# Agent attention on one core: v found and convolved one block further ahead, and the next image's moments with the third block

## The chip, the core and the metric

The kernel runs on one NeuronCore of a Trainium2 chip. The metric is the device time of one execution in microseconds. The engines are named as in the profile: PE multiplies matrices (PEld loads its weights), DVE is the vector engine, ACT the scalar engine, POOL is GpSimd, and SP issues DMAs. Matmul results lie in PSUM, everything else in SBUF. Each engine works through its own queue strictly in order; semaphores tie the queues together.

## The reference

Four layers, each `x = x + layer(groupnorm(x))`, on x of 32 images x 192 channels x 56 x 56 in fp32. Only the first layer is changed here, an attention through 49 "agents" with six heads of 32 channels:

```python
qkv = xf @ Wqkv + bqkv                       # xf: the normed image, 3136 pixels x 192
agent = q pooled 8x8                         # 49 agents
agent_attn = softmax(agent @ k.T * scale + pos_bias)   # over the 3136 pixels
agent_v = agent_attn @ v
q_attn = softmax(q @ agent.T * scale + agent_bias)     # over the 49 agents
out = q_attn @ agent_v + depthwise_conv3x3(v)
x = x + out @ proj_w + proj_b
```

The other layers (an RWKV scan, a shift with a 3 x 3 filter, a global convolution through spectra) follow it and are the same in both kernels.

## The kernel before

**Tiling.** `attention` (L365) takes the 32 images one after the other (loop over `b`, L759). The 56 x 56 pixels of an image are cut into four blocks of columns, 16, 16, 16 and 8 wide (`WIDTHS`); `j` counts them. The 192 channels lie as 128 and 64, and the 64 are folded by image halves onto 128 partitions, so each tensor is a pair (`_a`, `_c`).

**Pieces of work.** For the next image: `moments` (L433) takes the statistics and the 8 x 8 sums from the raw image, all on DVE (L438 to L461: `bn_stats`, then the reductions `by_x` at L447, `pool_a` at L450, `fours` at L455); `spread_of` and `scaling` make the group norm's scale of them; `normed` (L522) writes the normed block `xs_a`, `xs_c` on ACT; `find_agents` and `seen` (L495, L508) make the agents and what they see.

For a block: `find_v` (L538) computes v on PE and copies it on ACT into the padded images `v_a`, `v_c` (L546, L554) and into a flat tile. `convolve` (L560) applies the 3 x 3 filter: the centre tap on ACT (L570), the other eight as `scalar_tensor_tensor` on DVE (L572), for both tiles. Its right column needs the next block of v. `weigh` (L577) makes the scores of the 294 head-agent rows in three parts on PE (L585, L586), their row maxima `low` on DVE (L587) and the exponentials `pr` on ACT (L589). `turn_v` (L595) and `turn` (L608) transpose v and the exponentials through PE (L604, L617), with ACT copying (L605, L620). `gather` (L623) multiplies the two (L632, copied at L634) and `settle` (L637) turns the result and adds its halves (L641, L643, L645). `join` (L647 to L665) puts the four blocks together, almost all of it on DVE.

Then for each block `ask` (L669: scores on PE at L677 and L678, row maxima, subtraction and normalization on DVE at L681 to L694, exponential on ACT at L690), `turn_back` (L704, L708), `answer` (L712: L717, L722 on PE, sums with the convolved v on DVE at L719, L723) and `project` (L725, with matmuls in `_Pairs` at L834 to L847).

**What sets the order.** The order is that in which the functions are called, but a scheduler then moves instructions within each engine's queue by what it takes to be ready; the queues are fixed when the program is built. In the first loop over `j` (L766 to L781) the calls for a block are `weigh(j)`, `turn_v(j)`, `gather(j-1)`, `find_v(j+2)`, `turn(j)`, `settle(j-1)` and `convolve(j+1)`; after the last block come the next image's `moments`. In the second loop, over `t` = 1 to 5 (L788 to L812), `ask(t)`, `turn_back(t-1)`, `project(t-2)` and `answer(t-1)` run beside the next image's `normed`, `find_v(0)`, `find_v(1)` (at `t` = 3 and 4) and `convolve(0)`.

**PSUM.** All of this shares four tiles of two banks each (L379, L386). A matmul group that needs a tile waits until the copy or reduction that reads the tile's former contents is done.

**Words used.** low(j) are the three row maxima of block j; ask(1), turn(3) and so on are the calls for that block.

## Time and profile before

| | us |
|---|---|
| median of three runs | 12294.04 (12291.52 to 12297.86) |
| the profiled execution | 12294.66 |
| its span on the core | 12292.8 |
| PE busy | 11329.2 (92%) |
| DVE busy | 10836.4 (88%) |
| ACT busy | 6205.0 (50%) |

The span has the filter of the last layer first (until about 160 us), then the attention until about 4840 us, the scan in the middle and the spectra at the end. L653, one instruction an image, gives the period: from the 11th to the 12th image it runs at 1741.47 and 1888.23 us. One image in the trace, 1741.47 to 1888.24, has PE busy for 141.4 us, DVE for 127.4 and ACT for 81.2.

How to read what follows: a row of the timeline gives start, duration, engine, line, operation, output and inputs, the number of instructions merged, and in brackets the idle time ahead of it with what ended it. DVE's durations overlap their successors' by some 0.08 us, so sums are made of differences of starts. A row of the stretches gives the busy time of PE, PEld, DVE, ACT and POOL with counts, then the clock granted to PE (1.00 is full), the share of the DMA engines and GB/s.

### The profile page before, as it was taken

The numbers are of one execution on the slowest core, as the hardware profiler recorded it, in microseconds if no ns is written. First come the engines' busy times: TensorE is split into PE (matmuls) and PEld (weight loads), VectorE is DVE, ScalarE is ACT, GpSimd is POOL, SyncE is SP. The second block draws the span as 40 slices with busy tenths as digits, with TensorE's granted clock in tenths as the row PEclk, the third lists the DMA queues.
The fourth block names the chain that finished last, engine by engine and source line by source line (L and its number), as shares of the span: only waits on it lengthen the run. The fifth ranks groups of instructions, "written<-read, shape, count | busy, mean of one in ns | idle before, by whom it ended". The sixth has DMA issues, their size and how long they took to land. (4 is left out here: it accounts for less than half of the span.)

```text
span 12292.8 us, 164375 instructions
## 1 busy us (share of the span) xinstructions
PE 11329.2 (92%) x62734; PEld 7107.7 (58%) x62734; DVE 10836.4 (88%) x15489; ACT 6205.0 (50%) x11808; POOL 2250.7 (18%) x2228
## 2 busy tenths in 40 slices
PE   7999999999999999788888888888999999999999
PEld 3555555655555555333333333336777777777777
DVE  6888888888888887999999999997888888888888
ACT  3555555555555554566666666663333333333333
POOL 0000000000000000655555555551000000000000
PEclk9999999999999999999999999999999999999999
DMA  2111111111111111244344433442111111111111
GB/s 69 40 42 46 52 41 40 40 40 40 40 40 40 42 50 44 75 103 100 95 97 103 101 94 97 103 101 65 44 41 45 41 44 42 44 42 44 42 43 29
DMA packets 930055, 719.69 MB, mean 59 GB/s; under 512 B 770325, under 2 KB 807236, under 8 KB 920124
## 3 DMA queue, kind: packets, MB, share of 16 engines
q1 hardware_dynamic: 919020, 683.39, 21.7%
q10 hardware_dynamic: 10240, 25.70, 0.8%
q8 instruction: 500, 8.19, 0.3%
q14 instruction: 295, 2.42, 0.1%
HBM read 403.47 MB, written 240.65 MB: 52 GB/s over the span
## 5 line engine op out<-in xcount | busy, mean ns | idle before, releaser
L572 DVE SCALAR_TENSOR_TENSOR o<-v_a,att_w,o 128x896 f32<-128x896 f32 (+1 forms) x1024 | 1053.8, 1029 | 418.6 <-ACT v_a L546 291.5
L1763 ACT COPY y<-ps 64x252 f32<-64x252 f32 (+1 forms) x2376 | 808.2, 340 | 1135.0 <-PE ps L1757 1104.8
L1681 PE MATMUL ps<-fixed,real 84*84 84x112 f32 x6144 | 1090.9, 259 | 0.0
L1681 PE MATMUL ps<-fixed,imag 84*84 84x112 f32 x6144 | 1089.5, 259 | 0.0
L1688 ACT COPY z<-ps 84x448 f32<-84x448 f32 x768 | 405.6, 528 | 1218.5 <-PE ps L1681 1217.0
L1086 POOL MEMSET f<- 128x1 f32 x96 | 8.9, 99 | 4726.3 <-DMA st_c<-st 4721.3
L1681 PEld LDWEIGHTS ps<-fixed,real 84*84 84x84 f32 x6144 | 784.0, 153 | 134.2 <-issue 95.8
L1681 PEld LDWEIGHTS ps<-fixed,imag 84*84 84x84 f32 x6144 | 763.8, 153 | 0.0
L1079 ACT ACTIVATE q<-q 128x784 f32<-128x784 f32 x384 | 328.2, 855 | 802.5 <-DVE q L1074 633.1
L834 PE MATMUL ps<-sq,fixed 128*128 128x392 f32 x512 | 297.3, 743 | 428.6 <-ACT sq L1157 428.6
L572 DVE SCALAR_TENSOR_TENSOR o<-v_c,att_w,o 128x448 f32<-128x448 f32 (+1 forms) x1024 | 635.0, 620 | 5.1
L585 PE MATMUL ps<-xs_a,gk_a 128*98 128x448 f32 (+1 forms) x1536 | 637.1, 495 | 0.0
L589 ACT ACTIVATE pr<-ps,low 98x896 f32<-98x896 f32 (+1 forms) x384 | 352.3, 918 | 559.9 <-DVE low L587 559.9
L586 PE MATMUL ps<-xs_c,gk_c 125*98 125x448 f32 (+1 forms) x1536 | 631.6, 492 | 0.0
L1547 POOL TENSOR_TENSOR mat<-tap,tap 114x114 f32<-114x114 f32 x96 | 40.8, 425 | 3166.1 <-PE ps L1607 2313.2
L677 PE MATMUL ps<-gq_a,xs_a 128*112 128x294 f32 x1792 | 602.8, 417 | 19.2 <-DVE pq L682 19.2
L1698 PE MATMUL ps<-z,fixed 84*114 84x448 f32 x1536 | 608.8, 539 | 0.0
L834 PE MATMUL ps<-x,weights 128*128 128x392 f32 x1536 | 577.4, 519 | 27.5 <-DVE bv L1108 14.2
L678 PE MATMUL ps<-gq_c,xs_c 125*112 125x294 f32 x1792 | 594.5, 412 | 0.0
L1655 PE MATMUL re<-y,fixed 128*84 128x420 f32 (+1 forms) x1152 | 532.3, 543 | 8.7 <-ACT y L1763 7.6
L1655 PE MATMUL im<-y,fixed 128*84 128x420 f32 (+1 forms) x1152 | 526.9, 538 | 0.0
L690 ACT ACTIVATE pq<-pq 112x1176 f32<-112x1176 f32 x224 | 265.3, 1184 | 498.9 <-DVE pq L682 376.0
(367 smaller groups left out, 29245.2 us busy)
## 6 DMA issues: line engine op xcount, KB each, us to landing
x<-x SPq DMA_DIRECT2D x576, 392.0 KB
x<-x SPq DMA_DIRECT2D x512, 196.0 KB
x<-x SPq DMA_DIRECT2D x192, 399.0 KB
out_x<-x SPq DMA_DIRECT2D x384, 196.0 KB
x<-in_x SPq DMA_DIRECT2D x32, 1568.0 KB
x<-x SPq DMA_DIRECT2D x32, 1568.0 KB
x<-in_x SPq DMA_DIRECT2D x64, 392.0 KB
rd<-rd ACTq DMA_DIRECT2D x128, 196.0 KB
```

The lines of the kernel that those rows point to most:

```text
L572: nc.vector.scalar_tensor_tensor(dst, tap(i), dww[:, t, i : i + 1], dst, ALU.mult, ALU.add)
L585: mm(ps[P2, h, :n], g[:, cols], xs_a[j][:, px], start=True, stop=False)
L586: mm(ps[P2, h, :n], gk_c[0:KC, 2 * j + h, cols], xs_c[j][0:KC, px], start=False, stop=True)
L589: nc.scalar.activation(pr[:, :, :n], ps[P2, :, :n], AF.Exp, bias=low[:, j, p : p + 1], accum_out=sums[:, j, p : p + 1])
L677: mm(ps[:SUB, i, :HA], xs_a[j][:, px], g, start=True, stop=False)
L678: mm(ps[:SUB, i, :HA], xs_c[j][0:KC, px], gq_c[0:KC, 2 * j + (q + i) // ns], start=False, stop=True)
L834: mm(out, aa, srcs[t][h], start=True, stop=False)
L1655: nc.tensor.matmul(ps[:, : n * 84], f2[:, i, :], y[:, i0 : i0 + n].rearrange("p g s u -> p (g s u)"), start=True, stop=True)
L1681: nc.tensor.matmul(ps[:84, i * 2 * S : (i + 1) * 2 * S], part[:, i0 + i].rearrange("p s u -> p (s u)"), f3[:, m, :], start=(m == 0), stop= ...
L1688: nc.scalar.copy(z[:, i0 : i0 + n].rearrange("p g m w -> p (g m w)"), ps[:84, : n * 2 * S])
L1698: nc.tensor.matmul(got, f4[:, m, :], z[:, i0 : i0 + n, m, :], start=(m == 0), stop=(m == 1))
L1763: nc.scalar.copy(y[64 * m : 64 * m + 64, 2 * g0 + i : 2 * (g0 + n) : 2], got[64 * i : 64 * i + 64, :, :, m, :])
```

## The change

v of the next image is found for three blocks rather than two before its loop begins, its block 0 is transposed there, and its blocks 0 and 1 are convolved (the second call stands at `t` = 5). Within the loop, `turn_v` runs one block ahead of `turn`, `find_v` is left for block 3 alone, `convolve` runs two blocks ahead, and the moments are called with block 2 rather than block 3. The same instructions work on the same data.

```diff
     v, o = {0: find_v(0), 1: find_v(1)}, {}
-    o[0] = convolve(0)
+    vT = {0: turn_v(0, v[0])}
+    v[2] = find_v(2)
+    for j in range(2):
+        o[j] = convolve(j)
...
-            vT = turn_v(j, v[j])
             if j > 0:
-                halves = gather(j - 1, *turned[j - 1])
-            if j + 2 < NK:
-                v[j + 2] = find_v(j + 2)
-            turned[j] = turn(j, prs), vT
+                halves = gather(j - 1, turned[j - 1], vT[j - 1])
+            if j + 1 < NK:
+                vT[j + 1] = turn_v(j + 1, v[j + 1])
+            if j == 0:
+                v[3] = find_v(3)
+            turned[j] = turn(j, prs)
             if j > 0:
                 settle(j - 1, halves, got)
-            if j + 1 < NK:
-                o[j + 1] = convolve(j + 1)
-            elif more:
+            if j + 2 < NK:
+                o[j + 2] = convolve(j + 2)
+            elif more and j + 2 == NK:
                 mv, pools = moments(nxt)
-        halves = gather(NK - 1, *turned[NK - 1])
+        halves = gather(NK - 1, turned[NK - 1], vT[NK - 1])
...
             if more and t == 4:
                 o[0] = convolve(0)
                 normed(nxt, rs, nb, 3)
+            if more and t == 5:
+                vT[0] = turn_v(0, v[0])
+                v[2] = find_v(2)
+                o[1] = convolve(1)
```

## The prediction

> **What bounds the kernel now.** I read the page first, then one image in stretches, then PE's and DVE's rows in the stretches where PE is not full.

> ```profile
> span 12292.8 us, 164375 instructions
> PE 11329.2 (92%) x62734; PEld 7107.7 (58%) x62734; DVE 10836.4 (88%) x15489; ACT 6205.0 (50%) x11808; POOL 2250.7 (18%) x2228
> PE   7999999999999999788888888888999999999999
> DVE  6888888888888887999999999997888888888888
> ```

> The diff touches attention alone, some 250 to 4840 us: slices 2 to 16, PE at 9, DVE at 8. The image correction L653 runs once an image, at 1741.47 and 1888.23 in the trace, so an image takes 146.8 us; 32 of them make the stage. One image, busy times of PE, PEld, DVE, ACT, POOL, then the clock granted to PE:

> ```profile
> 1741.47:1745.87 4.40, 1.88 (x13) 1.44 (x13) 4.40 (x10) 0.34 (x2) 0.00 (x0) 0.94 0.00 0
> 1745.87:1752.47 6.60, 6.56 (x30) 5.08 (x32) 6.60 (x10) 3.77 (x4) 0.00 (x0) 0.52 0.01 2
> ...
> 1808.77:1827.77 19.00, 19.00 (x87) 10.10 (x85) 12.84 (x19) 10.31 (x22) 0.00 (x0) 1.00 0.83 258
> ...
> 1845.97:1861.27 15.30, 14.71 (x111) 9.42 (x110) 15.30 (x25) 8.61 (x18) 0.00 (x0) 1.00 0.01 1
> 1861.27:1870.27 9.00, 9.00 (x96) 7.87 (x94) 9.00 (x21) 4.93 (x13) 0.00 (x0) 1.00 0.01 2
> ```

> PE is full from weigh(0) to ask(0). It is empty at the head of turn_back(0), and runs the 6.6 us after that at half clock (0.52). DVE is full from j = 1 to the end of the weighing, and empty for a third of j = 0. PE's rows at the two idle places:

> ```profile
> 1742.30 0.98 PE L468 MATMUL ps<-mv,att_k 128*128 128x1 f32 x8
> 1745.79 4.69 PE L704 MATMUL ps<-att_k,pq 112*98 112x112 f32 x24 [2.52 <-DVE f L658]
> ...
> 1806.09 1.02 PE L834 MATMUL ps<-o,att_w 128*128 128x224 f32 x4 [1.06 <-DVE o L719]
> ```

> The rest of PE's idle time is 0.63 us ahead of ask(1), 0.59 at gather(1), 0.34 and 0.23 at two turn_backs: 5.4 us an image. DVE's rows:

> ```profile
> 1825.03 2.34 DVE L572 SCALAR_TENSOR_TENSOR o<-v_a,att_w,o 128x896 f32<-128x896 f32 x2 [5.89 <-ACT v_a L546]
> ...
> 1866.48 0.61 DVE L587 TENSOR_REDUCE low<-ps 98x1 f32<-98x448 f32 x1
> 1867.01 1.15 DVE L438 BATCH_NORM_STATS2 st_a<-x 128x6 f32<-128x448 f32 x2
> ...
> 1870.31 3.37 DVE L447 TENSOR_REDUCE by_x<-x 128x392 f32<-128x3136 f32 x1
> ...
> 1877.21 0.75 DVE L681 TENSOR_REDUCE mx<-ps 112x12 f32<-112x588 f32 x1
> ```

> Two things to see. First, DVE idles 5.89 us for block 2 of v. Second, most of the moments run after the last low, from 1867.01 to 1877.21, when PE needs nothing of DVE: it does gather(2), turn(3), gather(3) and the first part of ask(0), without a gap until 1880.4. They are nearly hidden there.

> **The change, part by part.** No instruction is added or dropped but a few of waiting; the sums of work stay. What counts is DVE's queue, which the order of the changed kernel's instructions shows.

> *1. find_v(2) and turn_v(0) ahead of weigh(0).* The 5.89 us, and 0.20 at 1811.8, go from DVE: 6.1 us.

> *2. Moments with block 2.* In the new order all of the moments but a one-row memset stand ahead of block 3's last two lows. What stood after the last low and now stands before it: bn_stats and aggregates 1867.01 to 1870.31, 3.30; L447 3.27 and 1.70; L450 0.76; L455 0.91; L458 0.13; in all 10.1 us (starts subtracted in the timeline, L645 left out).

> *3. So the last low comes later.* From 1798.77, where the taps of block 0 go on once v's block 1 is there, to 1867.01 DVE was busy 61.93 of 68.24 us. Its chain keeps this start. The last low ended at 1867.0; now 1867.0 - 6.1 + 10.1 + 0.2 (semaphore steps) = 1871.2. ACT's exponential behind it takes 0.1 + 0.6, and of turn(3)'s 12 transposes nine wait for it, 0.83: the settle behind them starts at 1872.7, where it was 1869.82. **PE's price: 2.9 us.** Part of it falls earlier, at j = 0: the first low(0) now stands behind fifteen of convolve(1)'s sixteen taps, some 7 us after PE has its scores. This state has rows already, in the first image, where low(0) stands behind a whole convolve:

> ```profile
> 201.58 0.87 PE L604 MATMUL ps<-att_k,v 128*112 128x128 f32 x6 [0.79 <-ACT once L518]
> 203.34 0.87 PE L604 MATMUL ps<-att_k,v 128*112 128x128 f32 x6 [0.89 <-ACT vT L605]
> ```

> After it ACT's queue (L516, L518, three exponentials of 0.99, two L605 of 0.68, find_v(3)'s six copies 1.90, L620 0.54: 7.4 us) is longer than PE's own 6.2 us (turn_v 1.36, find_v(3) 2.62, turn 2.19), so 1.3 to 1.9 us of the 2.9 are seen here and the rest, 1 to 1.6 us, at turn(3). They are not added: DVE's queue sets the sum.

> *4. The ask.* DVE is now idle when ask(0) begins, but that does not help. PE waits for a PSUM tile that the second subtraction of ask(1) frees. From the row maximum of ask(0)'s last pair to that subtraction DVE took 1881.50 to 1892.41, 10.9 us. In the new order the join's three long steps (L660 0.87, L664 1.40, L665 0.21) stand inside this stretch, and one row sum (1.29) is out of it: 11.8 us by its sixteen rows. The maximum was 1.5 us late behind PE and will be 0.9 us late behind that row sum. Net 0.3 us later. I keep the half clock as it is. Behind it DVE has 2.5 us less to do, which takes the 0.23 at turn_back(1).

> *5. DMAs and queues.* No issue is moved but with its function; the next image's 2.35 MB (1568 and twice 392 KB) land in 1808.77:1827.77 (share 0.83), before the earlier moments would need them (some 1855). SP and POOL have nothing else here.

> Sum for an image: 2.9 + 0.3 - 0.2 = 3.0 us. In the first image the scheduler had already put these moments ahead (162 to 177 us), and DVE's chain there has hardly an idle place (1.0): 0. The last image has no moments: about 1 us by j = 0. **30 x 3.0 + 1 = 91 us.** The profiled execution took 12294.66 us (span 12292.8, 1.9 around it), the median of the runs is 12294.04: 12294.7 + 91 = 12386.

> *Unknown costs.* Whether turn(3)'s new wait also throws the clock: the nearest rows are 1.06 us (L834: clock 1.00 after it) and 2.52 us (0.52 after it, for 6.6 us). Mine is 1 to 1.6, nearer the first: 0; the other end is half of 6.6, so +3.3 us an image, at most +100. The new DVE waits in the chain, for find_v(2)'s and find_v(3)'s copies, come out within 0.2 to 0.8 us of it: 0 to +1 us, taken 0.2. Should the ask's wait shrink by a few tenths and the clock lose less: -1.7 us (one half of the 6.6 us); taken 0.

> The row at 1745.87 has half clock after 2.52 us of idle. [...]

> **Rivals.** *Faster: the ask's wait goes.* For it: moments are off DVE when ask(0) begins, and DVE is up to 3 us late there now (1877.21 against the first pair's end near 1874.3). If DVE needed under 9.3 us (PE's own work from that pair to turn_back(0)) in place of 11.8, then 0.63 + 2.52 and the half clock (6.6 x 0.48 = 3.2) would go: -6.3 + 2.9 = -3.4 us, 31 times: 12190. Against: DVE's order is fixed, and a start with an empty queue does not shorten what stands behind the last pair.
> *No change:* DVE's 4.0 us net delay of the last low is taken up. PE's slack there is only 0.85 us (1868.76 against the exponential's end, 1867.91). It needs the tile waits and the ask to give back some 3 us: 12295, give or take 25.
> *Slower still:* the wait at turn(3) throws the clock: 12386 + 50 to 100, 12440 to 12490.
> That the change does not do what it says is excluded by the order of its instructions.

> **How the numbers follow.** Forecast as summed (12335 to 12430) 0.55; slower still 0.15; no change, within 0.2% (25 us, about what a measurement of this kernel can tell from none) 0.12; faster 0.18. So faster 0.18, same 0.12, slower 0.70. The range, 12280 to 12490, leaves out most of the faster case (0.16) and a little above.

> **What would show it.** Right: an image of about 149.8 us; no 5.89 at L572; L447 ahead of the last L587; DVE idle before the first L681; PE waiting 1 to 1.6 us for ACT's pr at L617 of block 3 and under 1 us twice at L604 of j = 0; 2 to 3.5 us still idle ahead of turn_back(0). Wrong: no wait at that L617, or full clock after turn_back(0).

## The result and the profile after

The changed kernel takes **12415.1 us** (median of four runs, 12403.0 to 12416.2) where the kernel before took 12293.7 beside it (12291.5 to 12297.9): ratio **1.0096, interval 1.0079 to 1.0114**. It is slower by 121 us; the forecast was 12386, slower by 91. The profiled execution took 12414.3 us.

The head of the page after; compare span, PE's and DVE's busy time, and slices 2 to 16:

```profile
span 12412.3 us, 164446 instructions
...
PE 11388.9 (92%) x62734; PEld 7121.4 (57%) x62734; DVE 10869.1 (88%) x15489; ACT 6177.0 (50%) x11808; POOL 2285.2 (18%) x2228
...
PE   6999999999999999888888888888999999999999
...
DVE  5888888888888888899999999997888888888888
```

Both engines do the same instructions in the same number, and the page looks as before. The time has to be looked for in one image. The timeline of PE after, where PE idles in an image or has to wait for ACT (the image whose ask(0) begins at 1474.86 and ends with the next ask(0) at 1624.38):

```profile
1495.16 1.02 PE L468 MATMUL ps<-mv,att_k 128*128 128x1 f32 x8 [2.48 <-DVE pq L682]
1497.19 3.04 PE L704 MATMUL ps<-att_k,pq 112*98 112x112 f32 x16 [1.01 <-DVE pq L682]
...
1514.46 1.74 PE L704 MATMUL ps<-att_k,pq 112*98 112x112 f32 x16 [0.99 <-ACT pqT L708]
1516.43 1.77 PE L842 MATMUL ps<-o,att_w 128*128 128x448 f32 x4 [0.23 <-ACT pqT L708]
...
1561.15 1.02 PE L544 MATMUL ps<-xs_a,att_w 128*128 128x448 f32 x2 [0.23 <-ACT vT L605]
...
1577.60 1.86 PE L604 MATMUL ps<-att_k,v 128*112 128x128 f32 x12 [0.79 <-ACT once L518]
...
1622.16 0.38 PE L617 MATMUL ps<-att_k,pr 98*112 98x98 f32 x2 [0.53 <-ACT pr L589]
1622.78 0.97 PE L617 MATMUL ps<-att_k,pr 98*112 98x98 f32 x9 [0.23 <-ACT pr L589]
```

The last three rows are the price in the weighing: at j = 0 and at turn(3). The rows at 1514 and 1516, in and behind turn_back(1), and the one at 1561, where find_v(2) waits for a copy of turn_v(0), are new and were not forecast. The 0.59 at gather(1) and the 0.63 ahead of ask(1) are gone. The timeline of DVE after, end of the weighing and beginning of ask:

```profile
1613.01 3.36 DVE L447 TENSOR_REDUCE by_x<-x 128x392 f32<-128x3136 f32 x1
...
1618.23 0.85 DVE L450 TENSOR_REDUCE pool_a<-by_x 128x49 f32<-128x392 f32 x1
1619.00 0.99 DVE L455 TENSOR_REDUCE fours<-by_x 64x49 f32<-64x196 f32 x2
1619.91 0.61 DVE L587 TENSOR_REDUCE low<-ps 98x1 f32<-98x448 f32 x1
1620.55 0.20 DVE L458 TENSOR_TENSOR pool_c<-fours 64x49 f32<-64x49 f32 x1
1620.68 1.14 DVE L587 TENSOR_REDUCE low<-ps 98x1 f32<-98x448 f32 x2
...
1627.99 0.77 DVE L681 TENSOR_REDUCE mx<-ps 112x12 f32<-112x588 f32 x1 [2.82 <-PE ps L678]
```

The moments stand ahead of the last lows, the 5.89 us at L572 is gone, and DVE now idles ahead of ask(0), where it is of no use.

To place the time I cut every image at three starts on PE: ask(0), turn_back(0), weigh(0). All figures are means in us over images 5 to 27 (counted from 0), except the period, a mean over the 29 intervals between the second ask(0) and the 31st. "Taps to last low" is DVE's chain of step 3 of the prediction, with the idle time in it. "Half" is time at half clock in an image.

| kernel | time | period | ask(0) to turn_back(0) | to weigh(0) | to next ask(0) | taps to last low (idle) | half | first ask(0) at |
|---|---|---|---|---|---|---|---|---|
| before | 12293.7 | 146.80 | 22.01 | 62.97 | 61.81 | 68.32 (6.09) | 6.5 | 254.2 |
| after | 12415.1 | 150.43 | 22.33 | 69.82 | 58.36 | 72.39 (0.23) | 6.4 | 272.2 |
| moments alone | 12683.8 | 159.28 | 24.09 | 63.43 | 71.76 | 78.47 (6.09) | 18.1 | 252.2 |
| v ahead alone | 12312.8 | 147.60 | 22.33 | 69.63 | 55.64 | 69.61 (1.07) | 5.9 | 249.1 |
| convolve late | 12493.6 | 153.66 | 24.21 | 69.54 | 59.84 | 73.20 (1.07) | 12.2 | 254.2 |
| moments with block 3 | 12400.2 | 150.20 | 22.33 | 70.40 | 57.46 | 71.27 (0.23) | 9.9 | 266.0 |

Wherever v is ahead, turn_v(0) and find_v(2) (1.36 and 4.76 us of PE) have moved from the third stretch to the second. Less these 6.12 us, the change costs 2.7 us in the weighing, 0.3 in the ask and 0.7 between turn_back(0) and weigh(0). The whole: the first ask(0) comes 18.0 us later, the next 31 intervals add 110.1 (3.1, 29 times 3.63, 1.6), and behind the last ask(0) 8.6 us are given back: 119.5 us of span.

### The profile page after: what moved, and what is told of

It reads as the page before. It is cut to its first block, busy times and chain, and to the rows that moved or that the text cites. A ratio compares the mean times of both kernels' runs of the same rounds, so it can differ in the third digit from the quotient of the medians.

```text
span 12412.3 us, 164446 instructions
## 1 busy us (share of the span) xinstructions
PE 11388.9 (92%) x62734; PEld 7121.4 (57%) x62734; DVE 10869.1 (88%) x15489; ACT 6177.0 (50%) x11808; POOL 2285.2 (18%) x2228
## 5 line engine op out<-in xcount | busy, mean ns | idle before, releaser
L572 DVE SCALAR_TENSOR_TENSOR o<-v_a,att_w,o 128x896 f32<-128x896 f32 (+1 forms) x1024 | 1055.3, 1031 | 235.1 <-ACT o L570 127.4
L572 DVE SCALAR_TENSOR_TENSOR o<-v_c,att_w,o 128x448 f32<-128x448 f32 (+1 forms) x1024 | 636.8, 622 | 5.1 <-ACT v_c L557 2.4
```

The costliest lines, as they stand in the source:

```text
L572: nc.vector.scalar_tensor_tensor(dst, tap(i), dww[:, t, i : i + 1], dst, ALU.mult, ALU.add)
```

## Experiments

My theory was that DVE's queue up to the last low sets the weighing, and that the tile freed by the second subtraction of ask(1) sets the start of turn_back(0). The rivals were that finding v early, or convolving it early, is itself what costs, and that moments cost nothing wherever they stand.

### The moments alone

```diff
-            elif more:
+            if more and j + 2 == NK:
                 mv, pools = moments(nxt)
```

This edit is made to the kernel before.

> The kernel before with the moments alone called with block 2; v, its turning and its convolution stay where they were, so DVE keeps its 5.89 us idle at L572. Theory (DVE's queue up to the last low sets the end): all 10.1 us of moments now stand ahead of the last low and nothing is taken out for it, so the last low comes 10.1 us later, 0.85 us of that is PE's slack, and with the ask's +0.1 an image takes some 9 to 10 us more: 30 images, 12560 to 12600 us. Rival (the moments are hidden wherever they stand, and early v is what costs): 12294, give or take 25.

Measured: 12683.8 us, ratio 1.0316 (1.0298 to 1.0333), slower by 388 us. DVE's chain grew from 68.32 to 78.47 us, by the 10.1 us of moments that the theory names; the rival that moments are hidden anywhere is dead. But the time is 84 us beyond my range. The timeline of PE and the stretches of this run at turn(3) show why (the columns of the stretches are busy PE, PEld, DVE, ACT, POOL, then the granted clock):

```profile
1680.23 0.57 PE L617 MATMUL ps<-att_k,pr 98*112 98x98 f32 x2 [6.97 <-ACT pr L589]
```

```profile
1671.00:1680.00 9.00, 2.24 (x48) 2.05 (x48) 8.95 (x12) 0.95 (x3) 0.00 (x0) 0.88 0.00 0
1680.00:1685.00 5.00, 4.58 (x19) 3.11 (x19) 2.19 (x10) 3.13 (x10) 0.00 (x0) 0.50 0.00 0
1685.00:1700.00 15.00, 15.00 (x74) 10.96 (x74) 9.59 (x12) 3.09 (x4) 0.00 (x0) 0.90 0.01 2
```

PE waits 6.97 us in one place, and what follows, turn(3), gather(3) and the head of ask(0), runs at half clock. From turn(3)'s first transpose to ask(0) takes 3.7 us instead of 1.8, and the ask 24.09 instead of 22.01. That is the mechanism of the prediction's rival "slower still", here as a fact.

### v ahead alone

```diff
     vT = {0: turn_v(0, v[0])}
     v[2] = find_v(2)
-    for j in range(2):
-        o[j] = convolve(j)
+    o[0] = convolve(0)
...
-            if j + 2 < NK:
-                o[j + 2] = convolve(j + 2)
-            elif more and j + 2 == NK:
+            if j + 1 < NK:
+                o[j + 1] = convolve(j + 1)
+            if more and j + 1 == NK:
                 mv, pools = moments(nxt)
...
                 vT[0] = turn_v(0, v[0])
                 v[2] = find_v(2)
-                o[1] = convolve(1)
```

> The changed kernel with convolution and moments back where they were: find_v(2) and turn_v(0) ahead alone. The last lows stand after the first L447 of the moments but ahead of the second one, L450 and L455. Theory (DVE's queue): 6.1 us out, 6.7 in ahead of the last low, within PE's slack of 0.85: nothing for the weighing; what is left is the ask's 0.3 and, if it comes with this order, the PSUM tile of turn_back(1) (1.0 to 1.6): 12320 to 12350 us. Rival (finding and turning v early is itself what costs, whatever the moments do): 12390 to 12415.

Measured: 12312.8 us, ratio 1.0014 (1.0005 to 1.0024). The weighing costs nothing (55.64 and 6.12, against 61.81), the ask 0.3, the stretch behind turn_back(0) 0.5. The rival is dead: v ahead by itself costs 17 us, 7 less than the least I had expected.

### The convolution late

```diff
-    for j in range(2):
-        o[j] = convolve(j)
+    o[0] = convolve(0)
...
-            if j + 2 < NK:
-                o[j + 2] = convolve(j + 2)
-            elif more and j + 2 == NK:
+            if j + 1 < NK:
+                o[j + 1] = convolve(j + 1)
+            if more and j + 2 == NK:
                 mv, pools = moments(nxt)
...
-                o[1] = convolve(1)
```

> The changed kernel with the convolution one block ahead only, as before; v ahead and the moments with block 2 stay. The low lines of j=0 then come without fifteen taps ahead of them, so the 1.57 us stall at j=0 goes. Theory (DVE's queue sets the sum; the same work stands ahead of the last low): what is not waited for at j=0 is waited for at turn(3), an image takes as long as in the changed kernel; only the first image may be up to 18 us shorter: 12395 to 12420 us. Rival (the taps ahead of low(0), that is the convolution two blocks ahead, are the price): 1.57 us an image less, some 12345 to 12365.

Measured: 12493.6 us, ratio 1.0161 (1.0144 to 1.0178). **Both theories fail**: convolving two blocks ahead, which makes the stall at j = 0, is worth 78 us. PE at turn(3), then the stretches there, in this run:

```profile
1633.85 0.38 PE L617 MATMUL ps<-att_k,pr 98*112 98x98 f32 x2 [3.09 <-ACT pr L589]
1634.61 0.57 PE L617 MATMUL ps<-att_k,pr 98*112 98x98 f32 x2 [0.39 <-ACT pr L589]
```

```profile
1637.00:1640.00 3.00, 2.92 (x17) 1.75 (x18) 0.00 (x0) 0.81 (x2) 0.00 (x0) 0.50 0.01 3
1640.00:1650.00 10.00, 10.00 (x51) 7.33 (x48) 6.03 (x8) 1.91 (x3) 0.00 (x0) 0.93 0.01 2
```

DVE in this run, where the first low of blocks 0 and 1 stands ahead of the taps and DVE waits for scores:

```profile
1581.01 1.09 DVE L587 TENSOR_REDUCE low<-ps 98x1 f32<-98x896 f32 x1 [0.80 <-PE ps L586]
...
1603.64 1.09 DVE L587 TENSOR_REDUCE low<-ps 98x1 f32<-98x896 f32 x1 [0.27 <-PE ps L586]
```

The same stretch of the changed kernel keeps full clock:

```profile
1624.00:1627.00 3.00, 3.00 (x30) 2.12 (x30) 0.35 (x1) 1.19 (x4) 0.00 (x0) 1.00 0.00 0
1627.00:1637.00 10.00, 10.00 (x43) 7.13 (x42) 8.09 (x11) 2.13 (x3) 0.00 (x0) 1.00 0.01 2
```

Two things make the 3.2 us an image. DVE waits 1.07 us in its chain instead of 0.23, so the last low is 0.8 us later. And PE's wait, which the changed kernel takes in two places, stands here in one, and the clock falls: 6.8 us an image at half clock at turn(3) and ask(0), none there in the changed kernel. I formed the second half of this into a run of its own.

### The convolution late, with work in the place of the wait

To the kernel above, four matmuls (eight records in the trace) are added ahead of turn(3)'s first transpose, into the tile that the transposes overwrite.

```diff
-    def turn(j, prs):
+    def turn(j, prs, fill=None):
...
             ps = psum()
+            if fill is not None and q == 0:
+                for h in range(4):
+                    mm(ps[P2, h % 2, :], fill[:, :PAIR], xs_a[0][:, 0:BANK], start=True, stop=True)
...
-            turned[j] = turn(j, prs)
+            turned[j] = turn(j, prs, gk if j == NK - 1 else None)
```

> The run with the convolution late (12493 us), and ahead of turn(3)'s first transpose four added matmuls of 512 columns into the same PSUM tile, whose result nothing reads: some 3.5 us of TensorE work where it waits 3.5 us. Theory (that long wait in one place throws the clock to half, which costs 3.8 us an image after it; the same wait in two places does not): the filler takes the wait's place, the clock stays full through turn(3) and ask(0): 12365 to 12400 us, below the changed kernel though it does more. Rival (the clock is not the cause; DVE's queue alone makes the difference): 12485 to 12510, or slower by what of the filler does not fit.

Measured: 12436.1 us, ratio 1.0113 (1.0097 to 1.013): 57 us less than without the added work. PE and the stretches at the same place:

```profile
1614.38 3.68 PE L616 MATMUL ps<-xs_a,gk_a 128*98 128x512 f32 x8 [0.56 <-ACT halves L637]
1617.89 1.46 PE L620 MATMUL ps<-att_k,pr 98*112 98x98 f32 x12
```

```profile
1608.00:1616.00 8.00, 7.44 (x72) 5.62 (x71) 7.99 (x10) 0.45 (x2) 0.00 (x0) 1.00 0.01 3
1616.00:1626.00 10.00, 9.93 (x63) 6.47 (x62) 4.86 (x15) 3.99 (x11) 0.00 (x0) 1.00 0.00 1
```

Here added work on PE made the kernel faster: the clock stays at 1.00 where it was 0.50. The ask is back at 22.33 us from 24.21. That much is shown. The size was off by 36 us and more: I had put the clock at 3.8 us an image and it gave 2.3 (153.66 to 151.37). The chain of DVE is as in the run before (73.21), and what is left against the changed kernel, 0.9 us an image, is about as much as DVE's added idle time at the lows (1.06 against 0.23); no run shows that it is the same.

### The moments with block 3 again

The changed kernel with `elif more and j + 1 == NK` ahead of `moments(nxt)`.

> The changed kernel with the moments called with block 3, as before the change; v and its convolution stay ahead. In the order that comes out, L438 to L450 still stand ahead of the last low, only L455 twice (0.91 us) and L458 (0.13) go behind it. Theory (DVE's queue up to the last low): the last low comes 1.0 us sooner, the 0.76 us at turn(3) goes nearly whole, the 1.57 us at j=0 stays: 0.7 to 1.0 us an image, 12383 to 12395 us. Rival (the place where the moments are called is the price, whatever the order): near 12300.

Measured: 12400.2 us, ratio 1.0082 (1.0065 to 1.0099). The last low comes 1.1 us sooner (72.39 to 71.27), the wait at turn(3) is gone, and the weighing takes 0.9 us less, all as expected. But the time fell by 15 us only: 6 of them in the first image, and 0.24 us an image. The rest went at turn_back(0) and turn_back(1), where much the same waits as in the changed kernel now bring 9.9 us of half clock an image instead of 6.4. The time is 5 us above my range, and the rival, near 12300, is dead. The last section has what the traces show of the half clock.

### The first image

Two runs change the first image alone. In the first, everything ahead of weigh(0) is as in the kernel before, and the missing block is convolved within j = 0:

```diff
-    vT = {0: turn_v(0, v[0])}
-    v[2] = find_v(2)
-    for j in range(2):
-        o[j] = convolve(j)
+    vT = {}
+    o[0] = convolve(0)
...
+            if b == 0 and j == 0:
+                vT[0] = turn_v(0, v[0])
+                v[2] = find_v(2)
...
+            if b == 0 and j == 0:
+                o[1] = convolve(1)
             if j + 2 < NK:
```

> The changed kernel, but its first image (up to ask(0)) in the order of the kernel before: only the first two blocks of v ahead of weigh(0), one convolved. Theory (the 18 us by which the first ask(0) is late are made ahead of the first weigh(0), which waits behind two convolutions, and nothing gives them back): 12392 to 12402 us. Rival (the loss is made up later, or comes from the first images' moments): 12410 to 12416.

Measured: 12409.2 us, ratio 1.0094 (1.0077 to 1.0111); first ask(0) at 264.4. Only 7.8 of the 18.0 us are gone, and the time is 7 us above my range and 1 us under the rival's: this edit still convolves two blocks within j = 0, so it decides nothing. In the second run v stays ahead and the first image convolves one block ahead throughout:

```diff
-    for j in range(2):
-        o[j] = convolve(j)
+    o[0] = convolve(0)
...
-            if j + 2 < NK:
+            if b == 0 and j + 1 < NK:
+                o[j + 1] = convolve(j + 1)
+            elif b > 0 and j + 2 < NK:
                 o[j + 2] = convolve(j + 2)
-            elif more and j + 2 == NK:
+            if more and j + 2 == NK:
                 mv, pools = moments(nxt)
```

> The changed kernel, but with one block convolved ahead of the first image and, in the first image alone, one block ahead in the loop; all other images as in the changed kernel. Theory (the 18 us of the first image are the two convolutions that stand ahead of the lows of j=0, and convolve(2) within it, not v and not the moments): first ask(0) at 254 us in place of 272, 12392 to 12400 us. Rival (v ahead is what delays the first image): first ask(0) near 264 to 272, 12408 to 12416.

Measured: 12394.2 us, ratio 1.0079 (1.0063 to 1.0096); first ask(0) at 251.0, 21.2 us sooner than in the changed kernel, and the time 20.9 us less. So the first image's loss is the convolution, as this theory said. In the changed kernel nothing can cover it there. DVE's first low, then PE's rows behind it, both of the changed kernel's first image:

```profile
220.53 3.09 DVE L587 TENSOR_REDUCE low<-ps 98x1 f32<-98x896 f32 x3
```

```profile
222.64 0.60 PE L551 MATMUL ps<-xs_a,att_w 128*64 128x224 f32 x4 [1.09 <-ACT v L548]
226.28 0.57 PE L617 MATMUL ps<-att_k,pr 98*112 98x98 f32 x2 [2.66 <-ACT pr L589]
227.26 4.17 PE L617 MATMUL ps<-att_k,pr 98*112 98x98 f32 x22 [0.41 <-ACT pr L589]
```

### The join moved out of the way of turn_back(0)

These runs ask whether the second subtraction of ask(1) sets the start of turn_back(0), and look for a faster kernel. The join is called within ask(1), behind its first half (its values are held until answer takes them):

```diff
-    def ask(j, g):
+    def ask(j, g, between=None):
...
             nc.vector.tensor_tensor(rows, rows, _bc(sm, [SUB, 4 * HEADS, AG]), ALU.mult)
+            if between is not None and q0 == 0:
+                values.append(between())
...
-        values = join(low, sums, got)
...
-                asked[t] = ask(t, gq)
+                asked[t] = ask(t, gq, (lambda: join(low, sums, got)) if t == 1 else None)
```

On the kernel with v ahead alone:

> v ahead alone (12312 us), and the join called between the two halves of ask(1), so that of its long steps only L660 (0.87 us), and no longer L664 (1.40) and L665 (0.21), stands ahead of the second subtraction of ask(1). Theory (this subtraction frees the tile that turn_back(0) waits for): the 3.5 us of idle PE ahead of turn_back(0) falls to about 1, the clock then stays full there (some 2.5 us more), less up to 1.5 us at answer(0) for values that come later: 3.4 to 4.9 us an image, 12160 to 12205 us. Rival (the wait only moves to answer(0)): 12300 to 12330.

On the changed kernel:

> The changed kernel with the join called between the two halves of ask(1). Theory as for v ahead alone with the same edit: 3.4 to 4.9 us an image less than the changed kernel: 12265 to 12310 us; the weighing's price (1.57 us at j=0, 0.76 at turn(3)) stays. Rival (the wait only moves to answer(0)): 12400 to 12430.

Measured: 12367.5 us, ratio 1.0056 (1.004 to 1.0073), and 12431.0 us, ratio 1.0107 (1.009 to 1.0124): slower than their bases by 55 and 16 us. The theory is right in its first half: turn_back(0) starts 2.3 us sooner (20.02 against 22.33). The rest is wrong, and the rival too. PE at turn_back(0) on the kernel with v ahead alone:

```profile
1464.33 0.94 PE L708 MATMUL ps<-att_k,pq 112*98 112x112 f32 x8 [1.20 <-DVE pq L684]
1466.31 1.49 PE L708 MATMUL ps<-att_k,pq 112*98 112x112 f32 x8 [1.03 <-ACT pqT L712]
1468.80 1.73 PE L708 MATMUL ps<-att_k,pq 112*98 112x112 f32 x8 [1.00 <-ACT pqT L712]
```

The wait does not go to answer(0). The second and third parts of turn_back(0) each wait for the copy of the part before; I take it that only one tile had come free. Three waits of some 1 us within 6 us bring 11.9 us of half clock an image (10.5 on the changed kernel), where one of 2.5 and one of 1 brought 5.9.

Next, gather(3) goes behind ask(0), and the last settle goes into ask(1) with the join, so that ask(0) begins sooner and fills DVE's idle time:

```diff
-        halves = gather(NK - 1, turned[NK - 1], vT[NK - 1])
         asked[0] = ask(0, gq)
-        settle(NK - 1, halves, got)
-        values = join(low, sums, got)
+        halves = gather(NK - 1, turned[NK - 1], vT[NK - 1])
+
+        def late():
+            settle(NK - 1, halves, got)
+            return join(low, sums, got)
...
-                asked[t] = ask(t, gq, (lambda: join(low, sums, got)) if t == 1 else None)
+                asked[t] = ask(t, gq, late if t == 1 else None)
```

On the kernel with v ahead alone:

> v ahead alone, with gather(3) behind ask(0) and both the last settle and the join between the two halves of ask(1). ask(0) is 2 us of PE sooner, and no long step of the join stands ahead of the second subtraction of ask(1). Theory: no idle PE ahead of turn_back(0) over 1 us and full clock after it, but values come some 2 us later than in the run with the join alone moved, which answer(0) sees: 12130 to 12220 us. Rival (values late by more than turn_back(0) lasts, the wait goes to answer(0)): 12260 to 12330.

On the kernel before, and on the changed kernel:

> The kernel before with the edit that was fastest so far (gather(3) behind ask(0), the last settle and the join between the halves of ask(1)). Theory: in the kernel before DVE is busy with the moments until 1877.2, after PE has ask(0)'s first scores, and none of the join's long steps stands ahead of the second subtraction of ask(1) as it is. So scores that come 2 us sooner buy nothing, PE's work is only moved into the wait: 0 to 1 us an image, 12262 to 12296 us. The edit needs the DVE time that finding v ahead frees. Rival (the edit is worth the same 2.5 us an image on any base): 12205 to 12225.

> The changed kernel with the same edit. DVE idles 4.5 us ahead of and in ask(0), so it should gain what v ahead alone gained (2.5 us an image): 12325 to 12355 us, still slower than before, since the weighing's price (1.57 us at j=0 and 0.76 at turn(3)) stays. Rival (with the wait ahead of turn_back(0) gone the change as a whole wins): under 12294.

Measured, in this order: **12231.6 us, ratio 0.9948 (0.9932 to 0.9965)**, faster than both kernels; 12492.7 us, ratio 1.0158 (1.0141 to 1.0175); 12363.5 us, ratio 1.0051 (1.0034 to 1.0068). PE at turn_back(0) and answer(0) in the fastest:

```profile
1432.96 0.95 PE L708 MATMUL ps<-att_k,pq 112*98 112x112 f32 x8
1434.91 0.97 PE L708 MATMUL ps<-att_k,pq 112*98 112x112 f32 x8 [1.00 <-ACT pqT L712]
1436.88 0.97 PE L708 MATMUL ps<-att_k,pq 112*98 112x112 f32 x8 [1.00 <-ACT pqT L712]
1438.85 1.72 PE L721 MATMUL ps<-pqT,values 98*64 98x448 f32 x8 [0.99 <-ACT pqT L712]
```

No wait stands ahead of turn_back(0), which begins 3.95 us sooner (18.38); three copies are still waited for, 1.9 of the 3.95 us are lost again behind it (71.51 to weigh(0), against 69.63), and half clock falls to 3.6 us an image. The run came out 12 us above its expected range. On the kernel before the edit loses 198 us, against both expectations. PE there:

```profile
1510.01 2.51 PE L721 MATMUL ps<-pqT,values 98*64 98x448 f32 x6 [5.36 <-DVE values L665]
```

There DVE still has the moments to do when ask(0) begins; the join ends behind ask(1)'s own steps, and answer(0) waits 5.36 us for its values; half clock rises from 6.5 to 13.7 us an image. So the edit needs the DVE time that v ahead frees, and the direction of that theory holds, but the loss is 6.8 us an image (146.80 to 153.56) where I had expected a gain of 0 to 1. On the changed kernel it gains 52 us, less than the 81 on v ahead alone and 8 short of the expected range, and the rival that the change then wins is dead; at turn_back(0) it has the same first start (18.38) but 7.7 us of half clock an image against 3.6.

## Why the prediction was right, and where it was not

The direction and the mechanism of the weighing hold; the time, 12415, is in the likeliest case's own range. Two terms were wrong, the gain at turn_back(1) and the first image, and luck had a part in two places, named below.

*Steps 1 to 3, DVE's chain.* DVE's idle time in the chain fell from 6.09 to 0.23 us, the moments came in ahead of the last lows, and the chain grew from 68.32 to 72.39, by 4.07 us where the sum gave 4.2. The run with the moments alone shows their term singly: 10.1 us more. The 6.1 us to be taken out were put down to find_v(2) and turn_v(0) alone; with v ahead alone 1.07 us of idle time stays, at the first lows of blocks 0 and 1, and the early convolution is what fills it. PE's price in the weighing is 2.7 us, forecast 2.9. It is split as said: j = 0 takes 1.57 us more than its matmuls (1.3 to 1.9 forecast), turn(3) some 1.4 more (1 to 1.6), and the old 0.59 at gather(1) is gone. As idle time alone the wait at turn(3) is 0.76 us, less than the 1 to 1.6 that was named as a sign, and L604 at j = 0 waits once, not twice.

*Step 4, the ask.* 22.01 to 22.33, the forecast's 0.3, and half clock stays (6.5 and 6.4 us an image), which is in part luck: with much the same waits it was 9.9 us with the moments at block 3. That the second subtraction of ask(1) sets it is shown by the join moved away: 2.3 us sooner. **The term that failed is the 0.2 us to be gained at turn_back(1).** The stretch from turn_back(0) to weigh(0) became 0.7 us longer, not 0.2 shorter: the old waits of 0.34 and 0.23 us at two turn_backs are gone, but the second part of turn_back(1) now waits 0.99 us for the copy of the first, and find_v(2), which stands here now, 0.23 for a copy of turn_v(0). The trace shows the waits and their releasers; for the first I take it that the scheduler gave this part the tile that the copy frees. That assignment was not tested by a run of its own. Moments alone and v ahead alone both have a wait of 1.0 there too.

*The first image.* I took 0, having looked at the moments and at DVE's idle time there. It costs 18.0 us: the second convolution stands ahead of the first low, and PE has no other work at that point. The run with one block ahead in the first image takes 20.9 us off.

*Unknown costs.* I took 0 for the clock at turn(3), and the changed kernel has full clock there. Step 3 had the price in two places, but not that this is what saves the clock. The wait is short because the early convolution puts the other half of it at j = 0; in the run with the convolution late it is 3.5 us in one place, and the clock is at half behind it (0.50 in 1637.00:1640.00).

*The sum.* Per image 3.63 against 3.0, the first image 18 against 0, and 8.6 us given back behind the attention. The stretch from the last ask(0) to the end takes 7486.7 us before and 7478.1 after, and 7476 to 7486 in the other runs; I have no cause for this. It is luck that it takes off some of what the sum lacked.

*Rivals.* "Faster" said that DVE's order is fixed and an empty queue ahead of ask(0) does not help. That was right for the change as it is; it helps once ask(0) is moved forward, as the fastest run shows.

## What to carry to other kernels

Ask of an engine that is full what stands in its queue ahead of the result that another engine waits for; moving work into an idle place is worth nothing when other work moves in ahead of that result. A wait was not paid at its length alone here (3.5 us in one place at turn(3) brought 6.8 us of half clock an image, and split in two it brought none there): where PE has to wait, look for work to put there, or split the wait into parts that lie far apart, before shortening it. Parts that lie close together need not help: with the join alone moved, three waits of some 1 us within 6 us brought twice the half clock (11.9 us an image against 5.9) of one of 2.5 and one of 1. And when a freed resource lies idle somewhere else (DVE ahead of ask(0)), the gain comes only from the next edit, which brings work forward to it.

## What the runs showed of the hardware

PE's, DVE's and ACT's queues ran in order: taken line by line (7551 stretches of one line among PE's matmuls, 6667 on DVE, 4978 on ACT), the trace before has the instructions in the order of the built program, up to the program's first branch, which comes behind the attention.

I laid this grid over the attention of all 14 traces (300 to 4700 us) and took PE's busy share in each window that ran at full clock, L468's one-column matmuls left out. Below 0.4 the next window was at half clock 365 times in 365; between 0.4 and 0.6 it was 204 in 355; above 0.6 not once in 16253. After a window at half clock that was busy under 0.8, the next stayed at half, 273 times in 273. The traces before and after alone have 58 in 58, 19 in 38, not once in 2371, and 12 in 12.

A wait of 1.06 us is 0.31 of a window, and with the rest of it busy no window of these traces was followed by half clock. One of 2.5 us that lies whole in one window leaves at most 0.27 busy, and every such window was. That the share is the cause is my reading of these counts and of the run with the added matmuls.

This also bears on my sizes at turn_back(0). What the waits there cost went with where the grid lay, and in the changed kernel this shifts from image to image: 3.41, 6.83 or 10.24 us of half clock came with the same waits. I took the changed kernel and the one with the moments at block 3 together, 30 images of each from the second on, by where in a window turn_back(0) begins. From 1.54 to 2.52 us into it 10.24 us of half clock follow in the image (30 of 30), from 2.54 to 3.12 us 6.83 (17 of 17), from 3.21 us over the window's end to 0.38 us 3.41 (9 of 9), and in the 4 images between, 6.83. The changed kernel begins turn_back(0) in the first of these ranges 2 times in 30. With the moments at block 3 it does 28 times, since its period, 150.20 us, is nearly 44 windows (150.19), so that the place hardly moves. That is where most of its gain went: by these counts the phase of the grid set the price here, and not the waits, which are much the same.

The two kernels with the last settle moved show it too. From 1.59 to 1.93 us into a window no half clock follows, in 15 images of 15 of the two, and they differ in how often they begin there (9 and 6 times in 30). So a range for the price of these waits had to allow for none to three windows of half clock. Some of the expected ranges above were missed by 5 to 36 us and others by more; the runs do not show how much of each miss is the phase.
